# Two of three images combined instead of one of two, and no residual by hand in the middle, in a grouped 3x3 convolution

## The chip, the cores and the metric

The kernel runs on one core of a Trainium2 chip. The metric is the time of one execution in microseconds (us). An execution is also recorded by the hardware profiler; its times are counted from the first instruction of the span.

The engines are called as in the profile: PE is TensorE (matmuls), PEld its weight loads, DVE is VectorE, ACT is ScalarE, POOL is GpSimd, SP is SyncE, which only issues DMAs.

## The reference

The input x is 160 images of 128 channels, 32x32, float32. Each image is normalised in 32 groups of 4 channels, convolved 3x3 with one of five sets of weights (the images are cut into five sets of 32), and added to x:

```python
act = jax.lax.conv_general_dilated(xb, w, window_strides=(1, 1), padding=[(1, 1), (1, 1)], feature_group_count=5, ...)
x = x + _L0_conv_ref(_gn(x), L0_conv_U)
```

The weights are quantised first: w = s1*floor(U/s1) + s2*floor((U - v1)/s2), with the steps s1 and s2 from the range of U over all sets. In units of s2 a weight is a small integer.

## The kernel before

**Split in two parts.** A normalised image is split in a high part in float16 and a low part, also in float16, so that two float16 products replace a float32 one. The weights are exact in float16.

**Two ways to convolve an image.** Both save products by treating two neighbouring rows or columns at once: from a pair of values and their sums and differences, four products with combined weights give two outputs. `combined` (L563) says how an image is done.

- A *combined* image takes sums and differences of neighbouring columns for both parts. GpSimd and VectorE form them from x before the scaling: `beside_pairs` (L613) has GpSimd subtract (L619, one quarter), `combine` (L596) has VectorE subtract (L602, two quarters) and add (L609, one), `outer_columns` (L586) has GpSimd fill the edge columns (L590). Then ScalarE scales the four quarters to the high part `vh` (L637, 2048 elements a partition) and VectorE forms the low part `vl` (L643). TensorE takes 24 matmuls: 12 in `sums_of_pairs` (L753), 12 in `main` (L777), all from L742.
- A *plain* image is normalised to `z`, by GpSimd in `beside_pairs` (L625) or, for the first image of a statistics group, by ScalarE (L552). ScalarE rounds it to `hi` (L560), VectorE forms `lo` (L650) and its sums and differences of rows (L663, L671, L672). TensorE takes 30 matmuls: the high part directly (L687, 18), the low part by pairs (L742, 12).

**One iteration of the main loop** (`run`, from L988) has, for image i, written in the order in which each engine's queue gets it:

- PE: `sums_of_pairs(i + 1)`, which fills the banks m2 and m1, then `main(i)`, which adds to the two banks `eo` of image i.
- DVE: the low part of image i + 2, steps of the next set's weights (`take(later, ...)`), a residual by hand if there is one, `pairs(i + 1)` (L799, L801: m1/2 + m2 and m1/2 - m2 into `eo`), then `combine(i + 4)` or another step.
- ACT: first measuring pass of image i + 14 (L201, sum), the residual of image i - 1 (L827), `leave(i + 1)` (L790, m2 out of PSUM), the high part of image i + 3 (L637 or L560), second measuring pass (L208, squares).
- POOL: `beside_pairs(i + 4)`, told by a dependency to start after the VectorE work that stands before `pairs(i + 1)`; the residual's DMA (L850); every eight images the statistics of a group (L227 to L230, L243 to L252); sums of finished weights (L502 to L504); `outer_columns(i + 4)`.
- SP: the store of a pair of images (L855) and the load of another (L426), in one queue.

m2 has one buffer, m1 and `eo` two, `v` two, `vh` three, `x` eleven pairs of images.

**Residual.** ScalarE copies `eo` to `sum` (L827), and a DMA from GpSimd's queue adds it to x in SBUF (L850). `by_hand` (L812) lists images for which VectorE adds `eo` to x instead (L844).

**Weights.** The 42 VectorE steps of a set's three columns (L101 to L127, L478) are taken one at a time during the set before, from its image 2 (image 4 in the first set); `run(later)` takes what is left at image 28 of the set. A finished column is turned by TensorE (L487), copied by ScalarE (L496) and summed by GpSimd; after the third column GpSimd forms `across`, the weights of combined images.

Of the kernel before, what the change touches and what calls it, by code (L numbers as in the profile page):

```python
# [22 lines left out]
LAST = 4  # L23
# [112 lines left out]
def last_of(steps, last=None):  # L136
    for last in steps:
        pass
    return last


def run(steps):

    while True:
        try:
            next(steps)
        except StopIteration as end:
            return end.value
# [106 lines left out]
def general_path(tc, keep, steps, x, u, out):  # L255
# [8 lines left out]
    with tc.If(far > 0), ExitStack() as ctx:  # L264
# [9 lines left out]
        for n in range(N_SETS):  # L274
            un = one.tile([P, C, TAPS], F32, tag="u", name=f"g_u{n}")
            nc.sync.dma_start(un, uv[n])
            wn = one.tile([P, C, TAPS], F32, tag="w", name=f"g_w{n}")
            k1, k2 = run(steps.quantise(one, un, f"g{n}", F32))
            nc.vector.tensor_scalar_mul(wn, k1, steps.s1)
            nc.vector.scalar_tensor_tensor(wn, k2, steps.s2, wn, ALU.mult, ALU.add)  # L280
# [37 lines left out]
class Main:  # L318
# [25 lines left out]
    LOAD_LEAD = 18  # L344
    STEADY = 7
    BY_VECTOR = (8, 10, 11, 14, 19, 24, 29, 34)
    FIFTHS = 126
    THIRDS = 146
    EARLY = 8
    FIRST = 3  # L350

# [211 lines left out]
    def combined(self, i):  # L563

        if i < self.STEADY or i >= self.imgs:
            return False

        if i < self.FIFTHS:
            return i % 2 == 1
        return (i - self.FIFTHS) % 5 % 2 == 0 if i < self.THIRDS else i % 3 != 1  # L570

    def by_scalar_too(self, i):

# [238 lines left out]
    def by_hand(self, i):  # L812


        if i < self.FIRST or i >= self.imgs - LAST:
            return True
        return i > self.BY_VECTOR[-1] - 4 and i % 8 == 7

    def residual(self, i):

# [38 lines left out]
    def run(self):  # L859
# [49 lines left out]
        def take(steps, count, last=None):  # L909
            for _ in range(count):  # L910
                last = next(steps, None) or last
            return last

        def measure(stage, *images):
            for i in images:
                self.measure(i, (stage,))
# [70 lines left out]
        later, turned = iter(()), []  # L987
        for i in range(self.imgs):  # L988
# [34 lines left out]
            if n + 1 < N_SETS:  # L1023
                if b == (2 if n == 0 else 0):
                    self.load_set(n + 1)
                if b == (4 if n == 0 else 2):
                    later = (s for col in self.COLS for s in self.make_column(n + 1, col))
# [3 lines left out]
            if i < self.FIRST:  # L1031

                if i == 0:
                    measure(0, 8, 9, 10)
                    self.normalise(4)
                    self.high_part(4)
                if i == 2:
                    self.leave(3)
                    self.normalise(5)
                    measure(1, 9)  # L1040
                    self.high_part(5)
                    self.pairs(3)
                    measure(0, 11)
                    self.low_part(4)
                    run(self.combinations(4))
                self.residual(j)
            else:

                last = None
                if self.combined(i + 2):  # L1050
                    last = last_of(self.low_combined(i + 2))
                elif i + 2 < self.imgs:
                    self.low_part(i + 2)
                    take(later, 1)
                    last = last_of(self.combinations(i + 2))
                last = take(later, i % 2, last)
                if i + 4 < self.imgs:
                    self.beside_pairs(i + 4, last)
                if i > self.FIRST and self.by_hand(j):
                    self.residual(j)  # L1060
                for k in by_scalar:
                    self.measure(k, (0,))
                if i > self.FIRST and not self.by_hand(j):
                    self.residual(j)
                    self.accumulate(j)
                part = i + 3 < self.imgs and not self.combined(i + 3)
                if i + 1 < self.imgs:
                    self.leave(i + 1)
                for st in ready:
                    st.deviations()  # L1070
                if part:
                    if self.by_scalar_too(i + 3):
                        self.normalise(i + 3)
                    self.high_part(i + 3)
                if self.combined(i + 3):
                    self.high_combined(i + 3)
                for k in by_scalar:
                    self.measure(k, (1,))
# [82 lines left out]
```

## Time and profile before

| | us |
|---|---|
| runs | 1012.46, 1020.29, 1014.58 |
| median | 1014.58 |
| profiled execution: time | 1012.46 |
| profiled execution: span, first to last instruction | 1010.8 |
| busy PE / DVE / ACT / POOL | 951.7 / 899.1 / 831.5 / 575.2 |

A busy time is the union of an engine's instructions. Groups in the profile's list have a count, the busy time, the mean of one in ns, and the idle time just before them with what ended it. A line of the waits has who waited for whom, the total in us, the number of times and the longest. A line of the timeline begins with start and duration. Matmuls are pipelined: one takes 376 ns from start to end, and the next starts before that.

The mean granted clock of TensorE was 0.992.

### The profile page before, as it was taken

How to read it: one execution, taken by the hardware profiler on the slowest of the kernel's cores; microseconds unless marked ns; L12 is line 12 of the kernel's file. 1: busy time of each engine (PE TensorE's matmuls, PEld its weight loads, DVE VectorE, ACT ScalarE, POOL GpSimd, SP SyncE). 2: the span in 40 equal slices, each digit the busy share in tenths (PEclk: the TensorE clock that was granted, in tenths of full speed). 3: DMA queues.
4: the chain of work that ended last, by engine and by line, in shares of the span. 5: the costliest groups of instructions: out<-in, count | busy, mean ns of one | idle time of the engine just before them, and what ended most of it. 6: DMA issues, size and time to landing. Idle time of an engine off the chain costs nothing.

```text
span 1010.8 us, 13191 instructions
## 1 busy us (share of the span) xinstructions
PE 951.7 (94%) x4504; PEld 441.5 (44%) x4504; DVE 899.1 (89%) x1175; ACT 831.5 (82%) x1154; POOL 575.2 (57%) x622
## 2 busy tenths in 40 slices
PE   2889999998999999989999999999999989999997
PEld 1434444444444444434444444444444434444443
DVE  7988999997998999788989897988999987979995
ACT  5768989898898988889889888897988978899551
POOL 4346575665646466655556565646465776456740
PEclk9999999999999999999999999999999989999999
DMA  9528899999997988988988989998989798997774
GB/s 360 196 89 232 219 271 257 267 254 254 270 307 185 306 224 266 246 258 236 258 243 242 260 264 245 280 258 257 242 250 285 206 255 212 276 250 208 182 201 157
DMA packets 65116, 245.85 MB, mean 243 GB/s; under 512 B 5008, under 2 KB 5008, under 8 KB 65040
## 3 DMA queue, kind: packets, MB, share of 16 engines
q1 hardware_dynamic: 45312, 173.09, 48.8%
q0 software_dynamic: 19728, 71.84, 37.1%
q8 instruction: 37, 0.61, 0.2%
q14 instruction: 39, 0.32, 0.1%
HBM read 89.19 MB, written 83.89 MB: 171 GB/s over the span
## 4 chain that ended last, share of the span: by engine, by line
ACT 25%; POOL 24%; PE 18%; DVE 16%; issue 15%; DMA 1%; POOLq 0%; DVEq 0%; ACTq 0%
ACT vh L637 7%; ACT junk L208 7%; PE eo L687 6%; PE eo L742 5%; POOL v L590 4%; ACT sum L827 4%; PE m L742 3%; POOL rstd L243 3%; POOL xt L850 3%; ACT m L790 3%; POOL v L619 2%; DVE lo L650 2%; DVE v L602 2%; DVE eo L799 2%; DVE eo L801 2%
## 5 line engine op out<-in xcount | busy, mean ns | idle before, releaser
L687 PE MATMUL eo<-hi,wt 128*128 128x496 f16 (+2 forms) x1386 | 369.3, 376 | 0.8 <-ACT wt L496 0.8
L742 PEld LDWEIGHTS <-wt 128*128 128x128 f16 x1884 | 184.1, 99 | 208.4 <-issue 0.9
L637 ACT ACTIVATE vh<-v,rstd 128x2048 f16<-128x2048 f32 x82 | 164.2, 2003 | 73.9 <-POOL v L590 73.5
L643 DVE SCALAR_TENSOR_TENSOR vl<-v,rstd,vh 128x2048 f16<-128x2048 f32 x82 | 193.0, 2354 | 33.1 <-ACT vh L637 32.5
L687 PEld LDWEIGHTS <-wt 128*128 128x128 f16 x1458 | 143.1, 99 | 165.9 <-issue 2.5
L619 POOL TENSOR_TENSOR v<-xt 128x512 f32<-128x512 f32 x82 | 85.7, 1045 | 209.1 <-DVE vl L643 52.9
L742 PE MATMUL eo<-vh,wt 128*128 128x496 f16 (+1 forms) x492 | 184.3, 375 | 0.0
L742 PE MATMUL eo<-vl,wt 128*128 128x496 f16 (+1 forms) x492 | 184.2, 374 | 0.0
L201 ACT ACTIVATE junk<-xt 128x1024 f16<-128x1024 f32 x152 | 160.6, 1057 | 19.2 <-DMA xt<-in_x_dram 15.7
L208 ACT ACTIVATE junk<-xt,mv 128x1024 f16<-128x1024 f32 x152 | 174.0, 1145 | 0.1
L742 PE MATMUL eo<-rows,wt 128*128 128x496 f16 (+1 forms) x450 | 171.4, 381 | 0.0
L742 PEld LDWEIGHTS <-across 128*128 128x128 f16 x984 | 97.0, 99 | 139.6 <-issue 27.7
L827 ACT COPY sum<-eo 128x1024 f32<-128x1024 f32 x137 | 141.9, 1036 | 15.9 <-PE eo L742 15.9
L590 POOL TENSOR_SCALAR v<-xt,ngm 128x64 f32<-128x64 f32 x82 | 120.4, 1469 | 59.5 <-DVE v L602 59.2
L850 POOL DMA_DIRECT2D xt<-sum x137 | 120.8, 881 | 2.8 <-issue 1.9
L790 ACT ACTIVATE m<-m 128x512 f32<-128x512 f32 x157 | 93.7, 597 | 26.7 <-PE m L742 20.6
L742 PE MATMUL m<-vh,across 128*128 128x496 f16 (+1 forms) x246 | 93.3, 379 | 21.2 <-ACT m L790 17.1
L625 POOL TENSOR_SCALAR z<-xt,ngm,rstd 128x1024 f32<-128x1024 f32 x53 | 62.9, 1187 | 64.5 <-DVE rows L672 55.5
L602 DVE TENSOR_TENSOR v<-xt 128x960 f32<-128x960 f32 x82 | 97.4, 1187 | 0.0
L650 DVE TENSOR_TENSOR lo<-z,hi 128x1024 f16<-128x1024 f32 x78 | 96.0, 1231 | 0.0
L742 PE MATMUL m<-vl,across 128*128 128x496 f16 (+1 forms) x246 | 93.5, 380 | 0.0
L799 DVE SCALAR_TENSOR_TENSOR eo<-m1a,m 128x512 f32<-128x512 f32 x78 | 54.3, 696 | 40.7 <-ACT m L790 36.8
(131 smaller groups left out, 1301.4 us busy)
## 6 DMA issues: line engine op xcount, KB each, us to landing
xt<-in_x_dram SPq DMA_DIRECT2D x78, 1024.0 KB, 9.6
out_dram<-xt SPq DMA_DIRECT2D x78, 1024.0 KB, 5.9
xt<-sum POOLq DMA_DIRECT2D x137, 512.0 KB, 6.2
u<-in_L_conv_U_dram SPq DMA_DIRECT2D x4, 576.0 KB, 10.9
xt<-in_x_dram SPq DMA_DIRECT2D x4, 512.0 KB, 9.7
range<-in_L_conv_U_dram SPq DMA_DIRECT2D x3, 576.0 KB, 7.9
out_dram<-xt SPq DMA_DIRECT2D x3, 512.0 KB, 2.7
u<-in_L_conv_U_dram SPq DMA_DIRECT2D x2, 288.0 KB, 3.1
```

What stands on the lines that cost most here:

```text
L201: self.nc.scalar.activation(junk, image, ACTF.Copy, scale=-1.0 / image.shape[1], accum_out=self.mv[:, j, 0:1],)
L208: self.nc.scalar.activation(junk, image, ACTF.Square, bias=self.mv[:, j, 0:1], accum_out=self.mv[:, j, 1:2],)
L590: self.nc.gpsimd.tensor_scalar(self.view(self.v[i], 0, (512 + W // 2 - 1, 2), (W // 2, H)), self.view(self.image(i), 1, (W - 3, 2), (W, H) ...
L602: nc.vector.tensor_tensor(self.view(v, 1, (511, 2), (half, H), (1, half - 1)), self.view(x, 1, (1, 2), (W, H), (2, half - 1)), self.view(x ...
L637: self.nc.scalar.mul(vh, self.v[i], st.rstd[:, j])
L643: yield self.nc.vector.scalar_tensor_tensor(vl, self.v[i], st.rstd[:, j], self.hi[i], ALU.mult, ALU.subtract)
L650: self.nc.vector.tensor_sub(lo[:, 1 : self.H + 1, :].rearrange("p h w -> p (h w)"), self.z.pop(i), self.hi[i].rearrange("p h w -> p (h w)"),)
L687: nc.tensor.matmul(self.bank(target, a)[:, first:end, c0:c1], self.wts[n, col][:, k, :], tile[:, s0 : s0 + 2 * (end - first) - 1 : 2, c0 + ...
L742: self.nc.tensor.matmul(out, weights, moving, start=start and j == 0, stop=False, skip_group_check=True)
L790: self.nc.scalar.mul(m2, self.m2_ps, 0.5)
L827: nc.scalar.copy(self.as_banks(i, self.sum[i]), self.flat(i, eo))
L850: self.nc.gpsimd.dma_start(self.image(i), self.sum.pop(i), accum_op=ALU.add)
```

## The change

Four places, all in `Main`:

```diff
-    FIFTHS = 126
-    THIRDS = 146
...
     def combined(self, i):
         if i < self.STEADY or i >= self.imgs:
             return False
-        if i < self.FIFTHS:
-            return i % 2 == 1
-        return (i - self.FIFTHS) % 5 % 2 == 0 if i < self.THIRDS else i % 3 != 1
+        return i % 3 != 1
...
     def by_hand(self, i):
-        if i < self.FIRST or i >= self.imgs - LAST:
-            return True
-        return i > self.BY_VECTOR[-1] - 4 and i % 8 == 7
+        return i < self.FIRST or i >= self.imgs - LAST
...
-                last = take(later, i % 2, last)
+                last = take(later, 1, last)
```

Before, images 7 to 125 are combined when odd (60 of 119), images 126 to 145 at three of five (12 of 20), the rest at two of three (10 of 14). After, all from 7 on are combined unless i % 3 is 1, 102 in place of 82. The 16 images 31, 39, ... 151 that VectorE added go through ScalarE and a DMA. The weight step before `pairs` is taken in every iteration instead of every second one; as before, a plain image brings a step beside its low part (image i + 2) and one after `pairs` (image i + 4).

In the program this makes 120 matmuls fewer. Of the plain images 13 instead of 25 are normalised by ScalarE (L552) and 45 instead of 53 by GpSimd (L625).

## The prediction

> **What bounds the kernel now.** I call an image that `combined` accepts *combined* (C), another one *plain* (U). First the page: engine shares, then the two rows that the change multiplies.
>
> ```profile
> PE 951.7 (94%) x4504; PEld 441.5 (44%) x4504; DVE 899.1 (89%) x1175; ACT 831.5 (82%) x1154; POOL 575.2 (57%) x622
> ...
> L643 DVE SCALAR_TENSOR_TENSOR vl<-v,rstd,vh 128x2048 f16<-128x2048 f32 x82 | 193.0, 2354 | 33.1 <-ACT vh L637 32.5
> ...
> L590 POOL TENSOR_SCALAR v<-xt,ngm 128x64 f32<-128x64 f32 x82 | 120.4, 1469 | 59.5 <-DVE v L602 59.2
> ```
>
> TensorE is at 94%, but four engines are close behind. So I go by stretches, cut where ScalarE evacuates m2 (L790, one per image): images 34 to 60 (half combined, weights of the next set prepared), 130 to 146 (three of five, no weight work), and one triple C, C, U near the end (measuring done).
>
> ```profile
> 251.30:406.60 155.30, 152.61 (x728) 70.83 (x726) 143.31 (x186) 136.42 (x193) 92.48 (x93) 1.00 0.92 259
> 831.80:925.40 93.60, 92.56 (x440) 42.86 (x438) 79.01 (x88) 84.27 (x116) 53.47 (x55) 1.00 0.92 256
> 956.70:973.20 16.50, 16.50 (x80) 7.59 (x79) 16.00 (x18) 8.54 (x8) 7.82 (x8) 1.00 0.68 195
> ```
>
> Columns: length, busy PE, PEld, DVE, ACT, POOL, granted clock, DMA share. PE fills all three: it is the bound. The last row gives the price of a matmul without a gap: a triple issues 24 + 24 + 30 = 78 matmuls in 16.50 us, 0.2115 us each. VectorE has only 8% to spare in the first row. Then the waits:
>
> ```profile
> ACT vh L637 <- POOL v L590: 73.5, 42, 3.9
> ...
> DVE eo L799 <- ACT m L790: 44.1, 46, 3.6
> ...
> ACT junk L201 <- DMA xt<-in_x_dram: 15.7, 8, 7.9
> ```
>
> The longest one is a hand-over VectorE (L602) to GpSimd (L590) to ScalarE (L637), used by combined images only. It costs little while PE is the bound; with more combined images it is what I have to watch. Last, what one step costs from start to start, since records overlap by 0.07 to 0.1 us: VectorE, ScalarE and GpSimd.
>
> ```profile
> 853.34 1.15 DVE L602 TENSOR_TENSOR v<-xt 128x960 f32<-128x960 f32 x1
> 854.40 0.75 DVE L609 SCALAR_TENSOR_TENSOR v<-xt,twice 128x512 f32<-128x512 f32 x1
> 855.07 2.35 DVE L643 SCALAR_TENSOR_TENSOR vl<-v,rstd,vh 128x2048 f16<-128x2048 f32 x1
> 858.12 0.70 DVE L799 SCALAR_TENSOR_TENSOR eo<-m1a,m 128x512 f32<-128x512 f32 x1 [0.70 <-ACT m L790]
> 858.85 0.70 DVE L801 SCALAR_TENSOR_TENSOR eo<-m1a,m 128x512 f32<-128x512 f32 x1
> ```
>
> ```profile
> 866.85 1.22 DVE L650 TENSOR_TENSOR lo<-z,hi 128x1024 f16<-128x1024 f32 x1
> 868.10 0.69 DVE L663 TENSOR_TENSOR rows<-lo 128x1024 f16<-128x1024 f16 x1
> 868.71 0.42 DVE L671 TENSOR_TENSOR rows<-lo 128x512 f16<-128x512 f16 x1
> 869.04 0.42 DVE L672 TENSOR_TENSOR rows<-lo 128x512 f16<-128x512 f16 x1
> 869.38 0.69 DVE L799 SCALAR_TENSOR_TENSOR eo<-m1a,m 128x512 f32<-128x512 f32 x1
> ```
>
> ```profile
> 857.97 2.00 ACT L637 ACTIVATE vh<-v,rstd 128x2048 f16<-128x2048 f32 x1
> ...
> 863.15 0.60 ACT L790 ACTIVATE m<-m 128x512 f32<-128x512 f32 x1
> ```
>
> ```profile
> 854.60 2.99 POOL L590 TENSOR_SCALAR v<-xt,ngm 128x64 f32<-128x64 f32 x1 [0.41 <-DVE v L602]
> ...
> 882.53 0.80 POOL L590 TENSOR_SCALAR v<-xt,ngm 128x64 f32<-128x64 f32 x1 [0.50 <-DVE v L602]
> ```
>
> The two L590 rows do the same work on 64 elements: in the first it lasted until L643, started beside it, had ended (857.42); in the second it got in first.
>
> **The change, part by part.** *Pattern.* Combined images go from 82 to 102. TensorE loses 20 x 6 = 120 matmuls: 120 x 0.2115 = 25.4 us, all of it on the path today. VectorE: a combined image takes L602 1.06 + L609 0.67 + L643 2.27 + pairs 0.73 + 0.61 = 5.34; a plain one 1.25 + 0.61 + 0.33 + 0.34 + 1.34 = 3.87. 20 x 1.47 = +29.4 us. ScalarE: L637 for L560, 20 x (2.003 - 1.044) = +19.2; and since fewer plain images open a group, 12 of the L552 go (12 x 1.24 = -14.9). GpSimd: 20 x (1.469 + 1.045), 8 L625 fewer, 16 issues more: +50.3 - 9.5 + 14.1 = +55 on 575.
>
> *No image by hand in the middle.* VectorE loses 16 x 1.22 = 19.5 (L844); ScalarE gains 16 x 1.036 = 16.6 (L827); the POOL queue gets 16 accumulating DMAs (L850, 0.88 to issue, 6.2 to land). Behind each issue stands the next L590; SP's store now waits for that landing instead of for L844, and the loads behind it on SP. The software queue's 37.1% of 16 engines over 137 transfers is 2.74 us of all engines per image; at a share of 0.92 that is bearable, and I take +1 us in all (0 to 8: ScalarE waited for loads 8 times, 15.7 us, mostly at the start).
>
> *Weight steps.* Still 42 per set, but five per triple instead of three per pair; the last column is done at images 28, 59, 90, 122 instead of 28, 60, 92, 124. A step is 0.57 us by its rows (fourteen of a column sum to 8.0), 0.50 start to start. The step now taken in every iteration stands before the pairs and before the wait of L619 and L625 (`beside_pairs`): 0.5 us later for them in half the iterations, and for the accumulating DMA queued behind them on POOL. Buffers add no wait: `v` has two, and of three neighbours only two are combined.
>
> *The new bound while weights are prepared.* Per triple: TensorE 16.50, plus 0.1 per image for the small statistics matmuls, 16.8. VectorE 2 x 5.34 + 3.87 + 5 x 0.50 = 17.05, with L643 held up 0.1 by L590 about 17.15, so 5.72 per image. VectorE passes TensorE. There is also a loop that half-and-half never has, since it needs two combined images in a row: pairs end; L602 and L609 of the second C, 1.73; L643 of the first C runs and L590 gets through only 0.15 after it, 2.45; ScalarE from L637 to the end of L790, 857.97 to 863.75, less 0.1 of start-up, 5.7 (two measuring passes and a sum lie between); pairs, 1.4; then L602, L609, the plain image's four, two steps, pairs, 6.65. Sum 17.9, or 5.98 per image. If L590 gets in first it is 2.2 shorter and doesn't bind. In the trace's eight second-of-two cases L590 took 0.80 five times; I take 5.72 + 3/8 x 0.26 = 5.82.
>
> On top come hitches: every eight images the group's small GpSimd operations (L243 2.03 us, L247 1.0) stand ahead of an L590, and each finished weight column puts three or six more there. Today images 34 to 60 lie 155.3/26 - 27 x 0.2115 = 0.26 per image above TensorE's own, of which 0.1 is small matmuls. I take 0.17 (bounds 0.05 and 0.25: not none, as these operations remain; not much over today's). So 5.99.
>
> The Trainium skill's "SBUF — State Buffer", section "Who interferes with whom", says that a VectorE instruction with two SBUF inputs and a GpSimd one that reads SBUF exclude each other for a whole instruction, the first to come winning. The 2.99 us row agrees; the 0.80 us rows don't follow from it where L609 held the port before. By that rule with VectorE always ahead, the loop would bind always and the sum would be about 1024.
>
> *Sum*, against the profiled execution (span 1010.8, time 1012.46; the median of the runs is 1014.58, 2.1 above). Weights in preparation: images 7 to 28 126.8, 34 to 60 155.3, 66 to 92 154.1, 98 to 124 153.6; 99 images in 589.8, 5.96 each. After: 99 x 5.99 = 593.0, +3. The other 40 (28 to 34, 60 to 66, 92 to 98: 38.1, 38.2, 38.2; 124 to 130: 41.1; 130 to 146: 93.6) took 249.2. There VectorE has no steps (4.85 per image) and TensorE binds: 5.50 + 0.1 + 0.2 = 5.80, 232; plus two stalls of 3 us where the combined weights (L502 to L504, 3.3 us) still precede an L590 (today at four set ends): 238, -11. With +1 for loads: -7. 1012.46 - 7 = 1005.5; on the median's level 1007.6, so 1008.
>
> **The rivals.** (1) *The matmuls saved arrive whole*: L590 always gets in first and VectorE's idle time is squeezed out: 99 x 5.82 + 236 = 812.2, -26.8, 988. For: TensorE is full in all three stretches. Against: VectorE's own 17.15 per triple.
>
> (2) *Slower: the loop.* L590 behind L643 of the first C each time, at images 9, 12, 15 and on. 99 x (5.98 + 0.23) + 40 x (5.63 + 0.23) + 6 + 1 = 856, +17, 1032. It decides once L590 is blocked in over about two of three cases and hitches are no longer absorbed (the loop has no slack for them). For: 2.99 three times; L637's 73.5 us of waiting. Against: 0.80 five times.
>
> (3) *Transfers bind*: 0.92 x 5.94 = 5.46 us of DMA per image, + 3/26 x 2.74 = 5.78; if no stretch exceeds 0.97, 5.95 per image: 139 x 5.95 + 6 = 833, -6, 1009.
>
> **How the numbers follow.** Forecast 0.42 (own range 997 to 1020, hitches 0.08 to 0.28), (1) 0.23, (2) 0.30, (3) 0.05. A measurement of this kernel tells about 1% from no change: 1004.4 and 1024.7 are the borders. Faster: nearly all of (1), 0.22, a quarter of the forecast, 0.11, a bit of (3): 0.34. Slower: 0.8 of (2), 0.24, a little of the forecast and of (3): 0.28. Between: 0.38. Range 984 to 1036: about a third of (1) and of (2) lies outside.
>
> **What would show it.** Right: PE near 926 busy, DVE near 909; in images 34 to 60 DVE over 95% and PE gaps before main products, period near 6.0; images 130 to 146 below 5.85. L590's mean between 1.5 and 2.1. Wrong towards (1): the period in 34 to 60 below 5.85 with PE full. Towards (2): L590 rows of 3 us at every image divisible by three, and L637's wait over 150 us. Towards (3): L201's wait over 30 us.

## The result and the profile after

| | before | after |
|---|---|---|
| runs, median of four (lowest to highest), us | 1015.67 (1012.46 to 1020.29) | 1048.96 (1043.12 to 1050.69) |
| profiled execution: time / span, us | 1012.46 / 1010.8 | 1050.69 / 1049.0 |

The ratio is 1.0314, with a 95% interval of 1.0256 to 1.0372: the change costs 3.1%. The forecast of 1008 us and its range, up to 1036, were both too low.

The page of the kernel after: engine shares and the groups of the hand-over. In after, `vh` is L633 (before: L637), `vl` L639 (L643), the edge columns L586 (L590), the sums L598 and L605 (L602, L609), `lo` L646 (L650), `pairs` L795 and L797 (L799, L801), `leave` L786 (L790), GpSimd's quarter L615 (L619), the residual's copy L821 (L827) and its DMA L844 (L850):

```profile
PE 942.2 (90%) x4384; PEld 430.2 (41%) x4384; DVE 915.2 (87%) x1139; ACT 852.6 (81%) x1158; POOL 653.8 (62%) x670
...
L633 ACT ACTIVATE vh<-v,rstd 128x2048 f16<-128x2048 f32 x102 | 204.1, 2001 | 89.2 <-POOL v L586 87.5
...
L639 DVE SCALAR_TENSOR_TENSOR vl<-v,rstd,vh 128x2048 f16<-128x2048 f32 x102 | 240.9, 2362 | 35.6 <-ACT vh L633 35.4
...
L586 POOL TENSOR_SCALAR v<-xt,ngm 128x64 f32<-128x64 f32 x102 | 165.0, 1618 | 66.6 <-DVE v L598 66.6
```

The 120 matmuls are gone (4504 to 4384), and TensorE went from 94% busy to 90%. No engine is full now. The busy times hardly tell more; the line of the page that does is the chain that ended last (the work followed back from the last instruction, each time to what released it), by engine. First before's, then after's:

```profile
ACT 25%; POOL 24%; PE 18%; DVE 16%; issue 15%; DMA 1%; POOLq 0%; DVEq 0%; ACTq 0%
```

```profile
POOL 24%; ACT 22%; DVE 21%; issue 14%; PE 11%; DMA 6%; POOLq 0%; SPq 0%; ACTq 0%; DVEq 0%
```

Only 18% of the chain lay on TensorE even before, while it was 94% busy. The prediction left this line out. Read that way, the time was set by hand-overs between ScalarE, GpSimd and VectorE, and after by them still more.

The same stretches as in the prediction, cut at the same images, 34 to 60 and 130 to 146 (columns: length, busy PE, PEld, DVE, ACT, POOL, clock, DMA share, GB/s), in after:

```profile
262.70:426.50 163.80, 149.48 (x693) 67.58 (x692) 146.44 (x178) 140.96 (x193) 107.12 (x103) 0.98 0.93 251
869.20:963.40 94.20, 90.42 (x429) 41.91 (x428) 78.39 (x84) 86.73 (x118) 62.01 (x58) 1.00 1.02 271
```

Images 34 to 60 take 163.8 us in place of 155.3, with PE busy for 149.5 of them and VectorE for 146.4: both wait. Images 130 to 146 take 94.2 in place of 93.6. Summed over all 99 images beside which weights are prepared, 589.8 became 628.2 (5.96 to 6.35 each); the other 40 stayed at 249.2 against 249.5. The whole loss lies in the weight stretches.

The granted clock also differs, 0.981 in after against 0.992. Between images 7 and 146 it is at half in five stretches of after, 30.7 us in all, each of which begins in or just behind a gap of TensorE of 2.4 to 6.5 us; in before there are two, 10.2 us. Images 92 to 98 hold one of them and took 41.8 us, 38.2 before:

```profile
624.40:666.20 41.80, 35.31 (x157) 15.86 (x156) 30.08 (x32) 32.52 (x45) 26.41 (x28) 0.92 0.89 242
```

In it the matmuls start 0.42 us apart instead of 0.21. So TensorE also worked at half speed for a while behind such a stall.

The waits in after:

```profile
ACT vh L633 <- POOL v L586: 87.5, 48, 6.6
...
DVE eo L795 <- ACT m L786: 58.7, 57, 3.6
DVE vl L639 <- ACT vh L633: 35.4, 32, 4.7
PE m L738 <- ACT m L786: 34.1, 21, 6.5
...
ACT junk L201 <- DMA xt<-in_x_dram: 22.1, 11, 7.3
...
PE m L738 <- DVE vl L639: 14.4, 15, 4.3
```

They are the links of one loop: GpSimd's edges late, so `vh` late, so `leave` behind it late, so VectorE's `pairs` and TensorE's m2 late. One turn of it, in three timelines of after (start, duration), GpSimd, VectorE and ScalarE:

```profile
357.46 2.98 POOL L586 TENSOR_SCALAR v<-xt,ngm 128x64 f32<-128x64 f32 x1 [1.70 <-DVE v L598]
```

```profile
356.20 1.15 DVE L598 TENSOR_TENSOR v<-xt 128x960 f32<-128x960 f32 x1
357.26 0.74 DVE L605 SCALAR_TENSOR_TENSOR v<-xt,twice 128x512 f32<-128x512 f32 x1
357.93 2.35 DVE L639 SCALAR_TENSOR_TENSOR vl<-v,rstd,vh 128x2048 f16<-128x2048 f32 x1
...
366.27 0.70 DVE L795 SCALAR_TENSOR_TENSOR eo<-m1a,m 128x512 f32<-128x512 f32 x1 [0.84 <-ACT m L786]
```

```profile
360.47 2.00 ACT L633 ACTIVATE vh<-v,rstd 128x2048 f16<-128x2048 f32 x1 [0.69 <-POOL v L586]
...
365.64 0.60 ACT L786 ACTIVATE m<-m 128x512 f32<-128x512 f32 x1
```

L586 starts at 357.46 on 64 elements a partition and ends at 360.44, just after L639 (360.28). `vh` starts at once, 360.47, `leave` ends at 366.24, `pairs` starts at 366.27 after 0.84 us of idle VectorE. Counted over all 51 combined images that follow a combined one (the second of two): L586 was blocked behind L639 in 25 (it ended 2.5 us after L605 in the mean), stood in GpSimd's queue behind statistics and sums of weights in 16 (3.7 us), and got in at once in 10 (0.17 us). Of the 51 first ones, 20 stood in that queue as well (3.3 us). (An edge is counted to the queue when GpSimd was busy until it started, though VectorE's L598 had ended.) Of `vh`'s 87.5 us of waiting, some 60 follow an edge from that queue and some 26 one that VectorE held up. The longest turn, image 95, on GpSimd, ScalarE and TensorE:

```profile
627.25 1.83 POOL L243 TENSOR_TENSOR rstd<-ve,mhalf 128x8 f32<-128x8 f32 x1 [0.83 <-ACT ve L239]
...
635.31 0.91 POOL L502 TENSOR_TENSOR across<-across,wt 128x384 f16<-128x384 f16 x1
636.19 0.38 POOL L586 TENSOR_SCALAR v<-xt,ngm 128x64 f32<-128x64 f32 x1
```

```profile
636.60 2.00 ACT L633 ACTIVATE vh<-v,rstd 128x2048 f16<-128x2048 f32 x1 [6.63 <-POOL v L586]
```

```profile
642.41 0.59 PE L738 MATMUL m<-vh,across 128*128 128x512 f16 x1 [6.49 <-ACT m L786]
```

From 627.25 to 636.19 GpSimd does statistics, the sums of a finished column and `across`; the edges behind them take 0.38 us.

### The profile page after: what moved, and what is told of

The parts are those of the page before. It is cut to its first block, busy times and chain, and to the rows that moved or that the text cites. A ratio compares the mean times of both kernels' runs of the same rounds, so it can differ in the third digit from the quotient of the medians.

```text
span 1049.0 us, 13044 instructions
## 1 busy us (share of the span) xinstructions
PE 942.2 (90%) x4384; PEld 430.2 (41%) x4384; DVE 915.2 (87%) x1139; ACT 852.6 (81%) x1158; POOL 653.8 (62%) x670
## 4 chain that ended last, share of the span: by engine, by line
POOL 24%; ACT 22%; DVE 21%; issue 14%; PE 11%; DMA 6%; POOLq 0%; SPq 0%; ACTq 0%; DVEq 0%
ACT vh L633 7%; POOL v L586 7%; ACT junk L208 6%; DVE v L598 4%; ACT sum L821 3%; PE eo L738 3%; PE eo L683 3%; DMA xt<-in_x_dram 3%; POOL rstd L243 3%; POOL v L615 3%; DVE lo L646 3%; DVE eo L797 3%; DVE eo L795 3%; POOL xt L844 2%; ACT m L786 2%
## 5 line engine op out<-in xcount | busy, mean ns | idle before, releaser
L633 ACT ACTIVATE vh<-v,rstd 128x2048 f16<-128x2048 f32 x102 | 204.1, 2001 | 89.2 <-POOL v L586 87.5
L683 PE MATMUL eo<-hi,wt 128*128 128x496 f16 (+3 forms) x1026 | 275.2, 379 | 1.3 <-ACT wt L494 0.9
L738 PEld LDWEIGHTS <-wt 128*128 128x128 f16 x1884 | 182.2, 99 | 223.1 <-DVE rows L668 11.9
L639 DVE SCALAR_TENSOR_TENSOR vl<-v,rstd,vh 128x2048 f16<-128x2048 f32 x102 | 240.9, 2362 | 35.6 <-ACT vh L633 35.4
L738 PE MATMUL eo<-vh,wt 128*128 128x496 f16 (+1 forms) x612 | 229.4, 375 | 2.4 <-DVE eo L797 2.0
L738 PE MATMUL eo<-vl,wt 128*128 128x496 f16 (+1 forms) x612 | 229.2, 375 | 0.0
L615 POOL TENSOR_TENSOR v<-xt 128x512 f32<-128x512 f32 x102 | 107.6, 1055 | 181.1 <-issue 59.4
L586 POOL TENSOR_SCALAR v<-xt,ngm 128x64 f32<-128x64 f32 x102 | 165.0, 1618 | 66.6 <-DVE v L598 66.6
L201 ACT ACTIVATE junk<-xt 128x1024 f16<-128x1024 f32 x152 | 160.7, 1057 | 25.7 <-DMA xt<-in_x_dram 22.1
L821 ACT COPY sum<-eo 128x1024 f32<-128x1024 f32 x153 | 159.8, 1045 | 25.2 <-PE eo L738 24.9
L683 PEld LDWEIGHTS <-wt 128*128 128x128 f16 x1098 | 108.5, 100 | 127.6 <-issue 6.3
L738 PE MATMUL m<-vh,across 128*128 128x496 f16 (+1 forms) x306 | 117.4, 384 | 39.3 <-ACT m L786 34.1
L844 POOL DMA_DIRECT2D xt<-sum x153 | 134.8, 881 | 4.6 <-ACT sum L821 1.7
L738 PE MATMUL eo<-rows,wt 128*128 128x512 f16 x330 | 125.8, 381 | 0.0
L598 DVE TENSOR_TENSOR v<-xt 128x960 f32<-128x960 f32 x102 | 121.1, 1187 | 0.0
L786 ACT ACTIVATE m<-m 128x512 f32<-128x512 f32 x157 | 93.7, 597 | 17.0 <-PE m L738 16.8
L795 DVE SCALAR_TENSOR_TENSOR eo<-m1b,m 128x512 f32<-128x512 f32 x79 | 54.7, 692 | 33.6 <-ACT m L786 31.5
L605 DVE SCALAR_TENSOR_TENSOR v<-xt,twice 128x512 f32<-128x512 f32 x102 | 79.0, 775 | 5.4 <-POOL twice L252 5.4
```

Of the source, the lines that this page charges most:

```text
L201: self.nc.scalar.activation(junk, image, ACTF.Copy, scale=-1.0 / image.shape[1], accum_out=self.mv[:, j, 0:1],)
L586: self.nc.gpsimd.tensor_scalar(self.view(self.v[i], 0, (512 + W // 2 - 1, 2), (W // 2, H)), self.view(self.image(i), 1, (W - 3, 2), (W, H) ...
L598: nc.vector.tensor_tensor(self.view(v, 1, (511, 2), (half, H), (1, half - 1)), self.view(x, 1, (1, 2), (W, H), (2, half - 1)), self.view(x ...
L615: ins = nc.gpsimd.tensor_sub(self.v[i][:, 1536:], odd, even)
L633: self.nc.scalar.mul(vh, self.v[i], st.rstd[:, j])
L639: yield self.nc.vector.scalar_tensor_tensor(vl, self.v[i], st.rstd[:, j], self.hi[i], ALU.mult, ALU.subtract)
```

## The experiments

"Images 34 to 60" and "130 to 146" are always the stretches cut at these images, W the sum over the 99 images with weights in preparation, N over the other 40. Each ratio is to before, measured beside it.

**1. Each part alone, added to before.** The pattern:

```diff
     def combined(self, i):
-        if i < self.FIFTHS:
-            return i % 2 == 1
-        return (i - self.FIFTHS) % 5 % 2 == 0 if i < self.THIRDS else i % 3 != 1
+        return i % 3 != 1
```

> The pattern of the change alone: two of three images combined, the 16 residuals by hand and the old weight steps kept. Loop theory (edges by GpSimd held up by VectorE, then ScalarE's high part, m2, pairs): most of the loss is here, 1030 to 1050 us against 1015 before. Theory that the 16 added copies and accumulating DMAs cost the time: no loss here, 985 to 1015. Theory that the additional weight step costs it: 1000 to 1020.

Measured: 1056.52 us, ratio 1.0392 (1.0354 to 1.0430). By hand:

```diff
-        if i < self.FIRST or i >= self.imgs - LAST:
-            return True
-        return i > self.BY_VECTOR[-1] - 4 and i % 8 == 7
+        return i < self.FIRST or i >= self.imgs - LAST
```

> Only the residuals by hand in the middle taken out, pattern and steps as before. Loop theory: within 0.7% of before, 1008 to 1022 us, since half-and-half has no two combined images in a row. Theory of the copies and DMAs: 1030 or more.

Measured: 1013.74, 0.9972 (0.9941 to 1.0003). The weight step:

```diff
-                last = take(later, i % 2, last)
+                last = take(later, 1, last)
```

> Only the weight step taken in every iteration, pattern and residuals as before. Loop theory: within 0.7% of before, 1008 to 1022 us. Step theory: 1025 or more.

Measured: 1011.47, 0.9960 (0.9937 to 0.9984). The pattern is the whole loss. Alone the other two gain 0.3% (not clear of no change) and 0.4%, and beside the new pattern the two may give back some 0.8% (1.0392 to 1.0314, intervals that overlap). (Without the extra step W is 613.0 but N 270.2, as 13 steps are left over at the first set's end and 11 at each of the others: images 28 to 34 then take 46.0 us, not 38.1.)

**2. The hand-over away: after with the edges on VectorE.**

```diff
-        self.nc.gpsimd.tensor_scalar(
+        self.nc.vector.tensor_scalar(
             self.view(self.v[i], 0, (512 + W // 2 - 1, 2), (W // 2, H)),
```

> The changed kernel with the edge columns (64 elements a partition, 102 instructions) formed by VectorE right after its own differences, so ScalarE's high part no longer waits for GpSimd. Loop theory: the loop loses its 2.4 us and the statistics no longer stand before it: 995 to 1020 us against 1049 of the changed kernel. Rival, VectorE's total work is the bound: 102 more VectorE instructions of about 0.2 us each, 1050 to 1070.

Measured: 1028.33, 1.0118 (1.0075 to 1.0161). 21 us come back, and 12 us over before remain. From this kernel, in order: the group of the moved operation, the windows of images 34 to 60 and 130 to 146, and the longest wait for a transfer:

```profile
L586 DVE TENSOR_SCALAR v<-xt,ngm 128x64 f32<-128x64 f32 x102 | 32.1, 315 | 0.0
```

```profile
263.40:416.30 152.90, 145.98 (x697) 67.77 (x695) 148.20 (x195) 141.13 (x193) 77.37 (x84) 1.00 0.97 261
842.30:937.50 95.20, 89.73 (x423) 41.06 (x422) 79.21 (x94) 86.52 (x118) 42.23 (x48) 1.00 1.00 265
```

```profile
ACT junk L201 <- DMA xt<-in_x_dram: 56.9, 37, 8.1
```

W is down to 600.5, but N rose to 252.0: the DMA share is 0.97 and 1.00, and ScalarE waits 37 times for loads, 56.9 us in all (22.1 in after, 15.7 before).

**3. The hand-over away, another way: the edges stay on GpSimd, behind `beside_pairs` of the same image**, so before VectorE's L598.

```diff
                     self.beside_pairs(i + 4, last)
+                    if self.combined(i + 4):
+                        self.outer_columns(i + 4)
...
                     self.combine(i + 4)
-                    self.outer_columns(i + 4)
```

> The changed kernel with GpSimd's edge columns moved: issued right behind GpSimd's subtraction, while VectorE reads PSUM in pairs, and before VectorE's differences, which now wait for them. Loop theory: L639 can no longer hold them up and the statistics no longer stand before them: 1010 to 1030 us, as with the edges on VectorE (1028) or a little less, since VectorE gets no work. If the wait only moves to VectorE's differences: 1035 or more.

Measured: 1026.87, 1.0111 (1.0078 to 1.0145), as experiment 2. So it is when the edges are formed that counts, not which engine forms them. Both edits take the edges out of the queue and away from VectorE's L639 at once, so they don't tell these two apart. The same group in its profile:

```profile
L586 POOL TENSOR_SCALAR v<-xt,ngm 128x64 f32<-128x64 f32 x102 | 38.3, 376 | 0.0
```

376 ns a piece on GpSimd when VectorE doesn't hold it up, against 1618 in after.

**4. After without the weight steps** (all sets use the first set's weights):

```diff
-        n, _ = self.place(i)
+        n = 0
...
-                    later = (s for col in self.COLS for s in self.make_column(n + 1, col))
+                    later = iter(())
```

> The changed kernel without the weight steps of sets 1 to 4; all images use set 0's weights, so that part of the result is left out. VectorE loses 168 instructions, some 84 us. Loop theory: the loop loses 1.0 us of 17.9 in the weight stretches, 5.6 to 5.9 per image everywhere, 1000 to 1020 us. If VectorE's total work were the bound: its 915 us fall to 830 and the time to about 975.

Measured: 1008.41, 0.9909 (0.9870 to 0.9949). That is 41 us less than after by the ratios, more than either way of forming the edges early gives. With the hand-over in place, the same 99 images still take 601.1, 6.07 each. This is above the 5.6 to 5.9 expected: without its two steps the loop of the prediction is 17.9 - 1.0 = 16.9 us, 5.63 per image. The edit leaves out the steps on VectorE and also the sums of finished weights on GpSimd, so it doesn't part the two.

**5. Before with the edges on VectorE**, the diff of experiment 2 on the kernel before.

> The kernel before with the edge columns formed by VectorE. Loop theory: half-and-half has no such loop, and only the hand-overs late behind statistics and weight sums go: 1005 to 1014 us. If the hand-over to GpSimd cost in every combined image: below 1000. If 82 more instructions on VectorE cost their time: 1020 to 1030.

Measured: 987.93, 0.9720 (0.9690 to 0.9750): the fastest of the kernels that do the whole work, and faster than both. Its page, by busy time and by chain, and images 34 to 60:

```profile
PE 945.8 (96%) x4504; PEld 441.3 (45%) x4504; DVE 914.0 (93%) x1257; ACT 832.1 (84%) x1154; POOL 484.1 (49%) x540
...
PE 71%; DVE 9%; issue 6%; ACT 6%; POOL 4%; DMA 4%; SPq 0%; POOLq 0%; DVEq 0%; ACTq 0%
```

```profile
248.60:400.50 151.90, 151.45 (x726) 70.89 (x727) 145.99 (x200) 136.31 (x193) 72.18 (x79) 1.00 0.97 272
```

TensorE is 96% busy against 94%, a small step, but the chain is 71% TensorE against 18%. So the hand-over cost 28 us in before too, though before never has two combined images in a row while weights are prepared. The expectation by the loop alone, 1005 to 1014, was wrong; the rival below 1000 came.

This bears on the whole account. With the edges early in both kernels the change costs 1.0118 / 0.9720 = 1.041, some 40 us, and not less than the 3.1% with late edges. The late edges slow both kernels, by 28 and 21 us. They explain a good part of why after takes 1049 us and not 1008, but not why it takes more than before.

**6. Transfers: experiment 2, and only the even images' accumulating DMAs.**

```diff
         if i in self.sum:
-            self.nc.gpsimd.dma_start(self.image(i), self.sum.pop(i), accum_op=ALU.add)
+            total = self.sum.pop(i)
+            if i % 2 == 0:
+                self.nc.gpsimd.dma_start(self.image(i), total, accum_op=ALU.add)
```

> The changed kernel with the edges on VectorE and only the even images' accumulating DMAs; the residual of the odd ones is left out. If late loads from busy DMA queues hold the rest of the loss: the stretch of images 130 to 146 falls from 95 to 90 us or less, L201 no longer waits, and the time is 1000 to 1015 against 1028. If VectorE's work holds it: no change, 1022 to 1032.

Measured: 996.23, 0.9806 (0.9774 to 0.9837), 32 us less than experiment 2 and a little less than expected, with 76 of these DMAs in place of 153. Images 34 to 60, 130 to 146:

```profile
260.40:411.20 150.80, 146.00 (x698) 67.76 (x695) 148.03 (x195) 141.93 (x194) 66.96 (x72) 1.00 0.73 218
820.30:909.10 88.80, 88.65 (x424) 41.50 (x423) 80.00 (x94) 87.23 (x119) 34.21 (x40) 1.00 0.75 226
```

The DMA share falls to three quarters. Images 130 to 146 become full of matmuls, 5.55 us each. In 34 to 60, 5.80 each, it is VectorE that is full now (148.0 of 150.8), not TensorE. The edit also spares GpSimd 77 issues of 0.88 us and the stores their wait for these transfers; no run parts that from the traffic.

**7. The same diff on after, with the hand-over in place.**

> The changed kernel with only the even images' accumulating DMAs (the odd ones' residual is left out), edges on GpSimd. If the hand-over loop holds the time by itself: 1035 to 1050. If the two losses add: 1012 to 1024, 32 us below the changed kernel.

Measured: 1038.97, 1.0230 (1.0201 to 1.0259). 8 to 10 us instead of 32, hardly clear of after's interval: while the hand-over sets the pace, the transfers have time.

**8. All three out: experiment 6 without the weight steps** (the diff of experiment 4).

> The changed kernel with all three suspects out: edges on VectorE, accumulating DMAs of even images alone (the odd images' residual is left out), no weight steps (set 0's weights for all). If the account is whole, TensorE alone is left: 5.6 per image over images 7 to 146, some 780 us instead of 824 without the last edit, time 950 to 965. If something else holds the loop, 975 or more.

Measured: 962.15, 0.9451 (0.9420 to 0.9482), 34 us less again. Images 34 to 60:

```profile
248.70:394.20 145.50, 144.66 (x691) 67.56 (x689) 129.75 (x155) 140.50 (x191) 56.96 (x66) 1.00 0.80 240
```

PE is busy for 144.7 of 145.5 us: 5.60 per image, against 5.84 in the same stretch of experiment 5, where TensorE was full with the old pattern. The difference, 0.24, is about what the matmuls saved come to, one per image in this stretch (27 to 26) at 0.21 us; the rest is the weights' own small matmuls, which this kernel leaves out. In the weight stretches TensorE's saving arrives here and in no other run. (That is a reading by stretches: before with the same three parts out wasn't run.)

**9. Three of five instead of two of three**, from image 7, edges on VectorE (before, with that diff and):

```diff
-    FIFTHS = 126
+    FIFTHS = 7
```

> The kernel before with edges on VectorE and three of five images combined from image 7 on, residuals by hand and weight steps as before. TensorE would need 5.6 to 5.7 per image, VectorE 5.5, the transfers up to 5.8. If the transfers don't bind before, 970 to 985, a gain on 988; if they or VectorE do, 985 to 1000.

Measured: 1010.66, 0.9935 (0.9912 to 0.9958), 23 us behind experiment 5. With `take(later, 1, last)` as well:

> Three of five combined with edges on VectorE (1011) and a weight step in every iteration. If the loss of three of five is the burst of steps left over at image 28 of a set (43 to 44 us for images 60 to 66 instead of 34): 985 to 1000. If it is VectorE's work while the weights are prepared: 1003 to 1015.

Measured: 1016.54, 1.0008 (0.9989 to 1.0028), another 6 us worse. Both are above what was expected, and a smaller share of combined images doesn't pay either.

**10. Two in a row without more of them**: before, still half of the images combined up to 125, but in pairs:

```diff
-            return i % 2 == 1
+            return i % 4 in (1, 2)
```

> The kernel before with the combined images up to 125 put in pairs (i modulo 4 is 1 or 2): 60 of 119 as before, so TensorE, VectorE and the transfers have the same work; only their neighbourhood changes. Loop theory: the loop takes 22.7 us of every four images, as much as TensorE's 22.85, and the late hand-overs are no longer absorbed: 1025 to 1050. If only the number of combined images matters: 1010 to 1020.

Measured: 1029.34, 1.0121 (1.0081 to 1.0161). And with the edges on VectorE:

> The same pairs with the edge columns on VectorE. Loop theory: the hand-over is gone and the pairs cost little: 985 to 1000 us, near the 988 of half-and-half with edges on VectorE. If two combined images in a row cost time for another reason (ScalarE's two long high parts in a row, say), the loss of the pairs stays: 1000 or more.

Measured: 1014.97, 0.9988 (0.9968 to 1.0008): 27 us above experiment 5, where a loop by GpSimd alone should have left nothing. Here my theory fell in part: two in a row cost something without GpSimd's edges. Both kernels once more without the weight steps, first alternate, then in pairs:

> Every second image combined, edges on VectorE (988), without the weight steps (set 0's weights for all sets). TensorE is the bound with and without: 975 to 986.

> Combined images in pairs, edges on VectorE (1015), without the weight steps (set 0's weights for all sets). If neighbours cost time because VectorE's long stretch (two combined images with steps) and TensorE's (two plain ones) can't be evened out: the 27 us between pairs and alternation shrink to less than 10, 978 to 990. If neighbours cost by themselves (ScalarE's two long high parts, a buffer): 1000 or more.

Measured: 975.85, 0.9602 (0.9569 to 0.9635), and 992.65, 0.9768 (0.9735 to 0.9801). The gap of 27 us shrinks to 17, between the two cases expected, so the weight steps seem to be part of it and not all. TensorE's waits name a second part. In experiment 5, in pairs with edges on VectorE, and in pairs without weight steps:

```profile
PE small L233 <- POOL dv L230: 2.0, 4, 1.2
```

```profile
PE small L233 <- POOL dv L230: 20.0, 15, 1.8
```

```profile
PE small L233 <- POOL dv L230: 10.6, 15, 1.2
```

Once for each group of statistics, TensorE itself stands before the group's small matmul until GpSimd has its input: 18 us more beside a gap of 27, and 9 beside one of 17 (in the alternate kernel without weight steps the same wait is 1.4). Groups have eight images and this pattern a period of four, so each group meets the same place of the pattern; with a period of three (after) the wait is 9.8 in all. That is a reading of the trace; moving the statistics against the pattern wasn't tried.

**11. How much of the hand-over is GpSimd's queue?** After, from image 40 on with statistics and sums of weights issued behind the edges:

```diff
-            for st in middle:
-                st.deviation()
-                st.scales()
...
                     self.outer_columns(i + 4)
...
+                if i >= 40:
+                    finish()
```

(`finish` holds the moved operations.)

> The changed kernel with the second half of the statistics and the weight sums issued behind the edge columns instead of ahead of them (from iteration 40 on); the edges stay on GpSimd. If the queue ahead of the edges makes the hand-over dear: 1028 to 1040, most of the 21 us that VectorE's edges gave. If VectorE's hold on them (25 of 51 second images, 2.5 us each) does: 1042 to 1052.

Measured: 1044.26, 1.0293 (1.0267 to 1.0318). At most some 5 us come back (the interval meets that of after, 1.0256 to 1.0372). That doesn't show that the queue is cheap: the moved operations now stand before the next image's edges. The waits of this kernel:

```profile
ACT vh L633 <- POOL v L586: 85.3, 49, 6.7
POOL v L586 <- DVE v L598: 71.0, 73, 2.4
```

`vh` waits hardly less: 29 edges still start straight behind other work of GpSimd's queue, and 51.7 of the 85.3 us follow them.

The traces of other runs tell more. Cut the weight stretches in turns of three images, from the `leave` of one second image to the next, 30 in all. In 15 of them one or both edges of after came from the queue:

| us per three images | after | experiment 2 | experiment 7 | experiment 6 |
|---|---|---|---|---|
| the 15 with an edge from the queue in after | 20.4 | 18.4 | 19.9 | 18.1 |
| the other 15 | 17.5 | 17.7 | 17.7 | 17.2 |

Early edges (after to experiment 2, or 7 to 6 with half of the DMAs) help the first kind by 2.0 and 1.7 us and the second by nothing and 0.5. So most of what the hand-over costs after is GpSimd's queue, and less is VectorE's hold on the edges. This compares turns and is not an experiment with the queue alone.

**12. The residuals by hand again**, in experiment 2:

```diff
-        return i < self.FIRST or i >= self.imgs - LAST
+        if i < self.FIRST or i >= self.imgs - LAST:
+            return True
+        return i > self.BY_VECTOR[-1] - 4 and i % 8 == 7
```

> The changed kernel with the edges on VectorE and the 16 residuals by hand put back: 16 accumulating DMAs fewer, 16 VectorE instructions of 1.2 us more. If busy queues hold what is left: 1012 to 1024 against 1028. If VectorE's work holds it: 1032 to 1045.

Measured: 1019.54, 1.0053 (1.0036 to 1.0070). Removing them costs 7 to 9 us here, while alone (experiment 1) it made no clear difference: 16 more accumulating DMAs matter here, where the DMA share is 0.97 to 1.00.

## Why the prediction was wrong

**The account.** Taken out one after the other, from the ratio 1.031 of after: without the late edges 1.012 (-21 us), without half of the accumulating DMAs 0.981 (-32), without weight steps 0.945 (-34). The order matters: out of after alone they give 21, 8 to 10 and 41 us. So undoing one leaves the next. The forecast priced all three, but each beside TensorE, not on top of each other.

**Hitches, 0.17: the term that failed most.** The forecast took GpSimd's statistics and weight sums ahead of an edge at 0.17 us per image, 0.25 at most, "not much over today's". Against its 5.99 per image the weight stretches are 628.2 - 593.0 = 35.2 us longer. In the 15 turns of three images (experiment 11) whose edges didn't come from GpSimd's queue after takes 17.5 us, 5.85 per image, close to the forecast's 5.82 before hitches; in the other 15 it takes 20.4, 6.79 per image. Over all that is 0.5 per image for hitches, half-speed matmuls behind a stall included. The turns with queued edges are 2.8 us longer than the others; with early edges (experiments 2 and 6) the same turns are still 0.7 and 0.9 longer, so some 2 of the 2.8 are the edges and the rest other work of these images.

**The loop: the right price, the wrong frequency.** "In the trace's eight second-of-two cases L590 took 0.80 five times; I take 5.72 + 3/8 x 0.26" failed as well. Eight cases were too few (two more in the same trace came late from the queue): from image 130 on after had 6 held and 2 at once, and in its 30 turns 14 held, 6 at once, 10 in the queue. At 14 of 20 the prediction's own price gives 5.90, some 8 of the 35.2 us (an estimate). The price holds: the 11 turns with both edges held up by VectorE and none queued took 17.8 us in the mean (16.6 to 19.2), against 17.9. Rival 2 came nearest, the edges being late in 41 of 51, but 16 of these by the queue, and its 0.23 for hitches was too little.

**The other 40 images, -11: wrong.** 249.5 measured in place of 238. Of these 11.5 us, 10.1 lie at the four ends of sets: 155.3 against 24 x 5.80 + 6 = 145.2. There are three stalls of `vh`, 4.7, 6.6 and 5.3 us at images 33, 95 and 128, where the forecast had two of 3 us for the combined weights. Without weight steps these ends take 137.8 (experiment 4), with half of the DMAs 155.7 (experiment 7): it is the weights' work and not the transfers. Images 130 to 146 are 1.4 above the forecast.

**Transfers, "+1 us in all".** In after that is not refuted: 77 fewer DMAs give 8 to 10 us, so 16 would be some 2 (an estimate, by number). With the edges early 16 cost 7 to 9 (experiment 12) and 77 cost 32. Together 35.2 + 11.5 - 1 = 45.7 us, and the miss on the profiled execution is 1050.69 - 1005.5 = 45.2; the 0.5 lies outside the stretches.

**TensorE's saving, 25.4 us: right by stretches, and covered.** Images 34 to 60 show it in experiment 8 and images 130 to 146 in experiment 6. "All of it on the path today" was wrong: before's chain had 18% on TensorE. The sign to look for, PE near 926 busy, was wrong too: 942.2. The same 4384 matmuls read as 942.2 us in after and as 933.8 in experiment 2; more than half of that difference is the clock (some 12 us and 8 us more of busy time in the half-speed stretches between images 7 and 146, an estimate from the busy time in them).

**VectorE's 5.72 per image: right.** With edges on VectorE, about 0.2 each from start to start (its rows at 343.99 and 344.18 in experiment 2), two in a triple, it would be 5.72 + 0.13 = 5.85; experiment 6, where VectorE is full, has 5.80.

**"It costs little while PE is the bound": wrong already for before.** Experiment 5 gets 28 us from one 64-element operation moved. PE at 94% was read as the bound; the chain, with PE at 18%, said otherwise. The Trainium skill ("Trainium Kernel Development and Optimization", section "Performance Expectations") says that matmul busy time is a poor measure of how near a kernel is to its roofline. The 942.2 us here, only 9.5 less for 120 fewer matmuls, agree.

**The rule on the shared port.** The Trainium skill's "SBUF — State Buffer", section "Who interferes with whom", named the price for the prediction: a GpSimd instruction that reads SBUF and a two-input VectorE one exclude each other for a whole instruction. The 25 blocked cases and the 376 against 1618 ns agree with it. Read as VectorE always ahead, which the page doesn't say, it put the sum at about 1024, nearer to the result than the count of eight rows. Who wins when two such VectorE instructions follow each other: here mostly VectorE, not always.

**Signs.** L586's mean, expected between 1.5 and 2.1, came at 1.62, and `vh`'s wait, expected over 150 us if the loop bound, at 87.5: neither told the cases apart. The duration leaves out the time in GpSimd's queue, and the loop's wait lies on several links (87.5, 58.7, 35.4, 34.1 above).

**What stays open.** Why after is slower than before, and not only slower than forecast. With early edges in both the change costs some 40 us; two combined images in a row cost 27 at an unchanged number of them (experiment 10), and the 16 DMAs 7 to 9 (experiment 12). Of the 27, some 10 go with the weight steps, and the trace shows 18 at the statistics matmul; these overlap, and no run takes the second away. The queue alone, without VectorE's hold, wasn't taken out either.

## What to carry to other kernels

Before multiplying the images that use a hand-over between engines, move the smallest operation of that hand-over to another engine or an earlier place in today's kernel, and see whether the time falls: here it fell by 2.8%, and told more than the change itself. When several limits lie within a few per cent, price the saving by the second and third limit, and take suspects out together until the saving shows. Read the chain beside the busy times: an engine that was 94% busy and had 18% of the chain was not the bound here.

## What the runs showed of the hardware

- A GpSimd operation on 128x64 elements took 376 ns in the mean by itself and 2.98 us beside VectorE's two-input L639 of 2.35 us; on VectorE the same one took 315 ns.
- Where VectorE went from two-input L605 to two-input L639 with no gap, the waiting GpSimd L586 got in between in 8 of 33 cases and was held to the end of L639, 2.35 us, in 25.
- One accumulating DMA of 512 KB landed in 6.9 us (median) with a DMA share of 0.97 to 1.00 and in 4.6 us at 0.73 to 0.75 (experiments 2 and 6, the second with half as many of them).
- The granted clock of TensorE was at half for 3.4 or 6.8 us at a time, in five places between images 7 and 146 of after, each beginning in or just behind an idle gap of 2.4 to 6.5 us; matmuls then started 0.42 us apart instead of 0.21.
